# Two layers of cross-attention and feed-forward: the beta add moved ahead of the output product, and the last chunk's exponentials summed on VectorE

## The chip, the cores and the metric

One core of a Trainium2 chip. The metric is the device time of one execution in microseconds (us); the time of a kernel is the median of several runs. Engines are named as in the profile: PE (TensorE, matmuls), PEld (its weight loads), DVE (VectorE), ACT (ScalarE), POOL (GpSimd), SP (SyncE, which issues transfers here).

## The reference, cut to what matters

There are 8 batches of 112 tokens of width 512, and a context of 375 rows for each batch. Four steps follow each other, each added to the tokens: a one-head attention over the context, a quantized feed-forward, an attention with 16 heads of width 32, and a feed-forward with integer weights. The change lies in the third:

```python
scores = clip(q @ k.T / sqrt(32), -50, 50);  masked positions get -50
probs  = exp(scores) / sum(exp(scores))           # over the 375 rows of the context
ctx    = probs @ v                                # 16 heads side by side: 512 wide
delta  = rs * (ctx @ Wo.T + bo)
delta  = (delta - mean(delta)) / sqrt(var(delta) + 1e-5) * ln_gamma + ln_beta
x      = x + delta
```

Then `x` is normalized again (the kernel's "4" names) and goes into the last feed-forward.

## The kernel before, in words

The 896 tokens lie in SBUF as 7 tiles of 128 (`xs[i]`). Up to about 235 us the kernel does the first attention, the first feed-forward and the queries of the second attention. From about 235 to 396 us it runs the second attention, and after that the last feed-forward. In the stage that is changed the order on every engine is the order in which the code emits: nothing is reordered, and each engine waits in place for what its next instruction needs.

The stage is a loop over 8 batches `b` and, in each, 3 chunks `c` of 125 context rows. One step does the following.

- `scores(b, c)`: 16 small matmuls (L905) into four PSUM banks named "s", one for each of four groups of heads. DVE clips each bank into an SBUF tile (L910, four instructions of 125x448) and ACT takes the exponential in place (L911). The pool of banks has four, so the next scores wait for these clips.
- `fill(1)`: one step of the keys (L194) or values (L203) of a later batch, one to three steps a batch. It goes into one of only two PSUM buffers of the pool `ps_mm`; ACT evicts it (L197, L205). The product with Wo and the transposes of `transpose4` take their buffers from the same pool in turn.
- `sums(...)` of the step before: 16 matmuls of the exponentials with the values (L931) into "num". With the last chunk come 8 matmuls with a matrix of ones (L926) into "den", which holds the denominators: four over the first chunk's tiles, to which the second chunk's have been added, and four over the last chunk's tiles. ACT copies both out (L937, L938).
- `add(b)`, at chunk 2: the second chunk's exponentials are added into the first chunk's tiles, four tiles of 125x448 (L897). For batches 0 to 6 POOL does it, for batch 7 DVE. There are three sets of four tiles, and batch `b`, chunk `c` uses set `(b + c) % 3`.
- `convert_integers()`, at most steps: one or two pieces of the integer weights of the last feed-forward, which a transfer brought into one of two buffers "raw", are squared by ACT (L880, for a check of their range) and converted by POOL (L882). Then SP issues the next loads (L869) into the buffers that become free.
- `divide(b - 1)`, at chunk 1, on DVE: reciprocals of the denominators (L947) and products with them (L948).

The second half of a tile's work, for tile `i = b - 2`, is spread over batches `b` and `b + 1`. At chunk 2 of batch `b` (from batch 2 on):

- `write4(b - 3)` on DVE (L837), for the tile before, whose four transposes on PE (L844) follow the product;
- `project_product(i)`: 8 records of matmuls with Wo (L803) into a buffer of `ps_mm`;
- `project_begin(i)`: DVE adds the bias out of PSUM (L809), takes mean and variance (L143, L144, L812), and POOL computes a reciprocal root in small steps (`rsqrt_pool`, L105 to L109), scales it (L815) and adds beta to the tokens (L816). DVE applies gamma (L817).

At chunk 0 of the next batch, after its clips, ACT and DVE evict the transposes (L847, L848), and `project_end(i)` adds the update to the tokens on DVE (L822, which needs L815's factor and L816's tokens), takes the moments (L824 to L827) and starts another `rsqrt_pool`.

In chunk 2 of a batch the emitted order is: POOL's `add(b)`, `convert_integers()`, scores with clips and exponentials, a fill, `sums` of chunk 1, `write4`, the product, `project_begin`, the transposes.

A last tile's `project(6)` stands early in the last feed-forward, whose gate and up products are the matmuls of L1045.

Of the kernel before, what the change touches and what calls it, by code (L numbers as in the profile page):

```python
# [36 lines left out]
B, T, D = 8, 112, 512  # L37
KC = D // P
S2, CK = 375, 125
NCK = S2 // CK  # L40
# [5 lines left out]
NR = P // HD  # L46
# [24 lines left out]
def two_layers(ctx: ExitStack, tc: tile.TileContext, x, ctxT, ctxN, mask0, mask1, w1, w2, w3,  # L71
               wq, wk, wv, wo, bq, bk, bv, bo, gamma, beta, rscale,
               wg, sg, wu, su, wd, sd, out):
    nc = tc.nc
# [22 lines left out]
    xs = [tokens[:, i, :] for i in range(NT)]  # L97

    def rsqrt_pool(v, y, name):

        bits = stat.tile([P, 1], I32, name=f"{name}_b")
        nc.vector.tensor_scalar(bits, v.bitcast(I32), 1, None, ALU.logical_shift_right)
        nc.vector.tensor_scalar(y.bitcast(I32), bits, -1.0, RSQRT, ALU.mult, ALU.add)
        h = stat.tile([P, 1], F32, name=f"{name}_h")
        nc.gpsimd.tensor_scalar(h, v, -0.5, 1.0, ALU.mult, ALU.mult)  # L105
        t = stat.tile([P, 1], F32, name=f"{name}_t")
        for _ in range(3):
            nc.gpsimd.tensor_scalar(t, y, y, h, ALU.mult, ALU.mult)
            nc.gpsimd.tensor_scalar(y, t, 1.5, y, ALU.add, ALU.mult)  # L109
# [26 lines left out]
    def moments(srcs, name):  # L136

        r = srcs[0].shape[0]
        mv = small[-1].tile([P, len(srcs), nc.vector.BN_AGGR_DIM], F32, name=f"{name}_mv",
                             bufs=buffers(name))[:r]  # L140
        for j, src in enumerate(srcs):
            bn = small[-1].tile([P, nc.vector.BN_STATS_DIM], F32, name="bn", bufs=4)[:r]
            nc.vector.bn_stats(bn, src)  # L143
            nc.vector.bn_aggr(mv[:, j, :], bn)  # L144
        return mv
# [15 lines left out]
    def load(pool, src, shape, name, queue=nc.sync, dtype=F32):  # L161
        t = pool.tile(shape, dtype, name=name)
        queue.dma_start(out=t, in_=src)
        return t
# [550 lines left out]
    beta_s = load(tailp, beta.to_broadcast([P, D]), [P, D], "beta", nc.gpsimd)  # L715
# [82 lines left out]
    updates = {}  # L798

    def project_product(i):  # L800
        updates[i] = ps = ps_mm.tile([P, D], F32, name="mm")
        for kc in range(KC):
            nc.tensor.matmul(ps, lhsT=qT[:, kc, i * P:(i + 1) * P], rhs=wo_s[:, kc, :],  # L803
                             start=(kc == 0), stop=(kc == KC - 1))

    def project_begin(i):

        d = tailp.tile([P, D], F32, name="d", bufs=2)
        nc.vector.tensor_add(d, updates[i], bo_s)  # L809
        mv = moments([d], "ln3")  # L810
        var = stat.tile([P, 1], F32, name="ln3_var")
        nc.vector.tensor_scalar(var, mv[:, 0, 1:2], rs2, LN_EPS, ALU.mult, ALU.add)  # L812
        f = stat.tile([P, 1], F32, name="ln3_f")
        rsqrt_pool(var, f, "ln3")
        nc.gpsimd.tensor_scalar(f, f, rs, 1.0, ALU.mult, ALU.mult)  # L815
        nc.gpsimd.tensor_add(xs[i], xs[i], beta_s)  # L816
        nc.vector.scalar_tensor_tensor(d, d, mv[:, 0, 0:1], gamma_s, ALU.subtract, ALU.mult)  # L817
        updates[i] = d, f

# [31 lines left out]
    with tc.tile_pool(name="work2", bufs=1, side="right") as work2, \  # L851
# [14 lines left out]
        def load_integers(count):  # L866
            for w, which, half, c, n in todo[:count]:
                raw = work2.tile([P, PIECE], I32, name="raw", bufs=2)[:, :n]
                nc.sync.dma_start(out=raw, in_=w[:, c:c + n])  # L869
                loaded.append((raw, which, half, c - HALVES[which][half], n))  # L870
            del todo[:count]

        def convert_integers():
            for raw, which, half, c, n in loaded:
# [15 lines left out]
        sets = [[work2.tile([P, KC, T], F32, name=f"e{i}{r}") for r in range(NR)]  # L890
                for i in range(NCK)]

        def add(b):
            add = (nc.gpsimd if b in ADD_POOL else nc.vector).tensor_add
            for r in range(NR):
                e, e1 = (sets[(b + c) % NCK][r][:CK] for c in range(2))
                add(e, e, e1)  # L897

        def scores(b, c):
            kT = kvs_of[b][0]  # L900
            ss = [ps_s.tile([CK, KC, T], F32, name="s") for r in range(NR)]
            for dc in range(KC):
                for r in range(NR):
                    rows = slice(r * HD, (r + 1) * HD)
                    nc.tensor.matmul(ss[r][:, dc, :], lhsT=kT[rows, dc, c * CK:(c + 1) * CK],  # L905
                                     rhs=qT[rows, dc, b * T:(b + 1) * T], start=True, stop=True)
            es = sets[(b + c) % NCK]
            for r in range(NR):
                e = es[r][:CK]
                nc.vector.tensor_scalar(e, ss[r], upper[:, c, b:b + 1], -CLIP, ALU.min, ALU.max)  # L910
                nc.scalar.activation(e, e, AF.Exp, scale=SC1)  # L911
            return es
# [3 lines left out]
        def sums(b, c, es):  # L916
            if c == 0:
                sums.num = ps_av.tile([P, KC, T], F32, name="num")
            num = sums.num
            v = kvs_of[b][1]  # L920
            if c == NCK - 1:
                den = ps_av.tile([P, KC, T], F32, name="den")
                added = sets[b % NCK]
                for k, of in enumerate((added, es)):
                    for r in range(NR):
                        nc.tensor.matmul(den[r * HD:(r + 1) * HD], lhsT=ones[:CK, :HD],  # L926
                                         rhs=of[r][:CK], start=(k == 0), stop=(k == 1))
            for dc in range(KC):
                for r in range(NR):
                    head = slice((4 * dc + r) * HD, (4 * dc + r + 1) * HD)  # L930
                    nc.tensor.matmul(num[r * HD:(r + 1) * HD, dc, :], lhsT=v[:, c, head],  # L931
                                     rhs=es[r][:CK, dc, :], start=(c == 0 and dc == 0),
                                     stop=(c == NCK - 1 and dc == KC - 1))
            if c == NCK - 1:

                rden = added[0]
                nc.scalar.copy(rden, den)  # L937
                nc.scalar.copy(qT[:, :, b * T:(b + 1) * T], num)  # L938
                rdens[b] = rden
# [10 lines left out]

        STEPS = [3, 3, 3, 3, 2, 3, 3, 3]
        ADD_POOL = range(B - 1)
        last, rdens, later = None, {}, []
        folding = fold_bias()
        counts = list(due.values())
        load_integers(counts.pop(0))
        for b in range(B):
            for c in range(NCK):
                if c == 2 and b in ADD_POOL:
                    add(b)  # L960
                if (b, c) in due:
                    convert_integers()
                    if counts:
                        load_integers(counts.pop(0))
                es = scores(b, c)
                if c == 2 and b not in ADD_POOL:
                    add(b)
                if c < STEPS[b]:
                    fill(1)
                if c == NCK - 1:  # L970
                    sums(*last)
                if (b, c) == (B - 1, NCK - 1):
                    over = tailp.tile([P, 29], F32, name="over")
                    nc.gpsimd.tensor_scalar(over, squares, WIDE, 1.0, ALU.is_gt, ALU.mult)
                if b == 0 and c > 0:
                    next(folding)
                if c == 0:
                    while later:
                        later.pop()()
                    if b >= 3:  # L980
                        project_end(b - 3)
                elif c == 1 and b >= 1:
                    divide(b - 1)
                elif c == 2:
                    turned = 3 <= b < 3 + GROUPS[0][1]
                    if turned:
                        write4(b - 3)
                    if b >= 2:
                        project_product(b - 2)
                    if b == B - 1:  # L990

                        hits = ps_s.tile([1, 29], F32, name="s")
                        nc.tensor.matmul(hits, lhsT=ones[:, :1], rhs=over, start=True, stop=True)
                        wide = tailp.tile([1, 1], I32, name="wide")
                        nc.vector.tensor_reduce(wide, hits, AX.X, ALU.max)
                    if b >= 2:
                        project_begin(b - 2)
                    if turned:
                        later.append(transpose4(b - 3, ps_mm, "mm"))
                if last and c < NCK - 1:  # L1000
                    sums(*last)
                last = b, c, es
# [202 lines left out]
```

## Time and profile before

| | before |
|---|---|
| median of 3 runs | 516.82 us (516.54 to 517.11) |
| the profiled execution's own time | 516.34 us |
| its span, first to last instruction | 514.2 us |
| granted TensorE clock, mean | 0.997 |
| PE busy | 502.5 us, 98% |
| DVE busy | 337.2 us, 66% |
| ACT busy | 252.8 us, 49% |
| POOL busy | 134.4 us, 26% |

Busy time by engine in the stage that is changed, from the trace in windows of about one batch each:

| window (us) | length | PE | DVE | ACT | POOL |
|---|---|---|---|---|---|
| 267.9 to 290 | 22.1 | 22.10 | 12.07 | 10.63 | 5.96 |
| 290 to 309 | 19.0 | 18.87 | 16.94 | 11.36 | 13.32 |
| 309 to 330 | 21.0 | 20.23 | 19.17 | 11.67 | 11.02 |
| 330 to 350 | 20.0 | 20.00 | 16.15 | 12.16 | 13.39 |
| 350 to 372 | 22.0 | 21.89 | 18.90 | 13.89 | 13.95 |
| 372 to 394 | 22.0 | 22.00 | 18.03 | 13.95 | 10.76 |

How to read it: shares are averages, and an engine off the chain of work that ends last may idle at no cost. PE's busy time counts a matmul from when it began to when its end is modelled, with waits inside a group of matmuls included. A line such as "L809 DVE" means line 809 of the kernel before. In a timeline the columns are start, length, engine, line, operation, output <- input, shape, how many were merged, and in brackets the idle time of the engine before it and what released it. One fp32 matmul leaves two records in the trace.

### The profile page before, as it was taken

What the parts mean: (1) busy time and instruction counts of PE and PEld (TensorE: products, weight loads), DVE (VectorE), ACT (ScalarE), POOL (GpSimd) and SP (SyncE); (2) the same over time, 40 slices, a digit from 0 to 9 for tenths busy, and PEclk for the clock granted to TensorE, in tenths of its full rate; (3) what the DMA queues carried; (4) which work ended last, traced back from release to release, by engine and by line L of the source; (5) the groups of instructions that cost most, each with busy time, mean ns of one, the idle gap of its engine ahead of it and who ended that gap; (6) DMA issues with size and microseconds to landing.
All of it is one profiled execution on the core that took longest, in us unless ns stands there. A gap on an engine that the chain in (4) does not pass through costs nothing.

```text
span 514.2 us, 8868 instructions
## 1 busy us (share of the span) xinstructions
PE 502.5 (98%) x3402; PEld 315.8 (61%) x3402; DVE 337.2 (66%) x815; ACT 252.8 (49%) x438; POOL 134.4 (26%) x221
## 2 busy tenths in 40 slices
PE   9999999999999999999999999999999999999995
PEld 6445554455545455696565565555555788889984
DVE  3552548767798987965676688986897753334432
ACT  0326656857565666236675366465665233103310
POOL 0000121110111064211551475674754430000000
PEclk9999999999999999999999999999999999999998
DMA  8998795200120100122421112012320000010001
GB/s 241 347 407 326 268 324 205 80 18 0 61 82 1 60 2 0 45 101 61 162 68 51 62 52 62 3 53 62 98 69 13 20 1 1 20 42 20 1 20 48
DMA packets 13489, 45.77 MB, mean 89 GB/s; under 512 B 2097, under 2 KB 3392, under 8 KB 12288
## 3 DMA queue, kind: packets, MB, share of 16 engines
q1 hardware_dynamic: 11888, 41.43, 23.5%
q0 software_dynamic: 1248, 3.70, 2.2%
q8 instruction: 29, 0.48, 0.4%
q14 instruction: 20, 0.16, 0.1%
q10 hardware_dynamic: 304, 0.01, 0.0%
HBM read 41.46 MB, written 1.84 MB: 84 GB/s over the span
## 4 chain that ended last, share of the span: by engine, by line
PE 47%; DVE 6%; POOL 2%; ACT 1%; DMA 1%; issue 1%; DVEq 0%; POOLq 0%; ACTq 0%
PE s L1045 14%; PE mm L203 8%; PE down L1067 7%; PE mm L803 3%; PE s L905 3%; PE num L931 2%; PE mm L194 2%; DVE e L910 2%; PE den L926 2%; PE mm L740 1%; PE mm L738 1%; DMA raw<-in_wd_dram 1%; PE s L744 1%; DVE e L947 1%; ACT e L911 1%
## 5 line engine op out<-in xcount | busy, mean ns | idle before, releaser
L203 PE MATMUL mm<-wv,cT 128*125 128x512 f32 x192 | 87.6, 599 | 0.0
L194 PE MATMUL mm<-cT,wk 128*128 128x375 f32 x256 | 87.3, 485 | 0.0
L1045 PE MATMUL s<-h4T,w 128*128 128x512 f32 (+1 forms) x352 | 72.6, 367 | 0.2 <-PE num L931 0.2
L1045 PEld LDWEIGHTS s<-h4T,w 128*128 128x128 f32 x352 | 63.5, 188 | 8.8 <-PE num L931 0.4
L910 DVE TENSOR_SCALAR e<-s,upper 125x448 f32<-125x448 f32 x96 | 59.0, 677 | 14.7 <-PE s L905 13.9
L911 ACT ACTIVATE e<-e 125x448 f32<-125x448 f32 x96 | 51.6, 570 | 27.8 <-DVE e L910 27.3
L194 PEld LDWEIGHTS mm<-cT,wk 128*128 128x128 f32 x256 | 46.8, 190 | 27.6 <-issue 1.0
L203 PEld LDWEIGHTS mm<-wv,cT 128*125 128x125 f32 x192 | 34.5, 187 | 38.0 <-issue 36.4
L897 POOL TENSOR_TENSOR e<-e,e 125x448 f32<-125x448 f32 x28 | 33.1, 1213 | 15.8 <-PE num L931 15.8
L1067 PE MATMUL down<-w,gu 128*128 128x512 f32 (+1 forms) x176 | 37.0, 367 | 0.0
L541 PE MATMUL mm<-w_q,q_qT 128*128 128x512 fp8e4 (+1 forms) x168 | 34.8, 361 | 0.8 <-DVE tokens L583 0.4
L439 POOL DMA_DIRECT2D tokens<-x x14 | 10.7, 768 | 90.3 <-DVE x L433 63.0
L1067 PEld LDWEIGHTS down<-w,gu 128*128 128x128 f32 x176 | 29.8, 188 | 5.7
L880 ACT ACTIVATE w<-raw,zero_point 128x640 fp32r<-128x640 int32 (+2 forms) x29 | 22.6, 781 | 20.4 <-DMA raw<-in_wd_dram 9.2
L1053 ACT CAST gu<-gu 128x512 fp32r<-128x512 f32 (+1 forms) x22 | 12.5, 568 | 39.6 <-DVE gu L1051 39.6
L570 POOL TENSOR_SCALAR q<-gu 128x704 bf16<-128x704 f32 x14 | 10.8, 790 | 79.8 <-ACT gu L567 79.8
L882 POOL TENSOR_SCALAR w<-raw 128x640 fp32r<-128x640 int32 (+2 forms) x29 | 20.7, 724 | 36.0 <-ACT w L880 35.8
L905 PE MATMUL s<-qT,kv 32*125 32x112 f32 x768 | 29.4, 280 | 0.6 <-DVE qT L748 0.3
L1051 DVE SCALAR_TENSOR_TENSOR gu<-s,su,gu 128x512 f32<-128x512 f32 (+1 forms) x22 | 15.1, 684 | 21.8 <-PE s L1045 20.6
L905 PEld LDWEIGHTS s<-qT,kv 32*125 32x125 f32 x768 | 24.5, 183 | 7.1 <-issue 5.8
L541 PEld LDWEIGHTS <-q_qT 128*128 128x128 bf16 x168 | 16.3, 98 | 19.7 <-issue 2.5
L931 PEld LDWEIGHTS num<-e,kv 125*32 125x32 f32 x768 | 18.4, 110 | 13.6 <-issue 7.9
(238 smaller groups left out, 798.6 us busy)
## 6 DMA issues: line engine op xcount, KB each, us to landing
cT<-in_ctxT_dram SPq DMA_DIRECT2D x13, 750.0 KB, 6.1
raw<-in_w_dram SPq DMA_DIRECT2D x6, 1408.0 KB, 20.3
cN<-in_ctxN_dram SPq DMA_DIRECT2D x8, 768.0 KB, 4.5
raw<-in_wg_dram SPq DMA_DIRECT2D x8, 320.0 KB, 3.0
raw<-in_wu_dram SPq DMA_DIRECT2D x8, 320.0 KB, 2.9
raw<-in_wd_dram SPq DMA_DIRECT2D x8, 320.0 KB, 3.1
out_dram<-d SPq DMA_DIRECT2D x6, 256.0 KB, 2.0
wk<-in_wk_dram SPq DMA_DIRECT2D x4, 256.0 KB, 4.9
```

The source lines that it names most:

```text
L194: nc.tensor.matmul(ps[dc], lhsT=wk_s[:, kc, dc * P:(dc + 1) * P], rhs=cT[:, kc, :], start=(kc == 0), stop=(kc == KC - 1))
L203: nc.tensor.matmul(ps, lhsT=cT[:, kc, c * CK:(c + 1) * CK], rhs=wv_s[:, kc, :], start=(kc == 0), stop=(kc == KC - 1))
L541: nc.tensor.matmul(ps[:, :n], lhsT=qT[:, kc, :], rhs=w[:, kc * H + n0:kc * H + n0 + n], start=(kc == 0), stop=(kc == KC - 1))
L880: nc.scalar.activation(t, raw, AF.Square, bias=zero_point, accum_out=squares[:, k:k + 1])
L882: nc.gpsimd.tensor_scalar(t, raw, -128.0, 1.0, ALU.add, ALU.mult)
L897: add(e, e, e1)
L905: nc.tensor.matmul(ss[r][:, dc, :], lhsT=kT[rows, dc, c * CK:(c + 1) * CK], rhs=qT[rows, dc, b * T:(b + 1) * T], start=True, stop=True)
L910: nc.vector.tensor_scalar(e, ss[r], upper[:, c, b:b + 1], -CLIP, ALU.min, ALU.max)
L911: nc.scalar.activation(e, e, AF.Exp, scale=SC1)
L931: nc.tensor.matmul(num[r * HD:(r + 1) * HD, dc, :], lhsT=v[:, c, head], rhs=es[r][:CK, dc, :], start=(c == 0 and dc == 0), stop=(c == NCK ...
L1045: nc.tensor.matmul(ps[:, :n], lhsT=w[:, c:c + P], rhs=h4T[k][:, kc, :n], start=(kc == 0 and k == 0), stop=(kc == KC - 1 and k == 1))
L1067: nc.tensor.matmul(ps, lhsT=gus[k][:, hc, j * P:(j + 1) * P], rhs=w[:, c + n0:c + n0 + n], start=(hc == 0 and k == 0), stop=(hc == HC - 1 ...
```

## The change

Two edits. First, the POOL instruction that adds beta to a tile of tokens moves from `project_begin`, where it followed the reciprocal root, to the head of `project_product`, so that it stands on POOL ahead of the reciprocal root and is issued while the product runs.

Second, in batches 2 to 6 DVE adds the last chunk's exponentials into the tiles that hold the first two chunks' sum (`add_last`, four instructions of 125x448 for each batch, ahead of `project_begin`), and the four ones-matmuls over the last chunk's tiles are left out: the denominator is then one set of four matmuls instead of two. Batches 0, 1 and 7 keep theirs.

```diff
     def project_product(i):
+
+        nc.gpsimd.tensor_add(xs[i], xs[i], beta_s)
         updates[i] = ps = ps_mm.tile([P, D], F32, name="mm")
...
         nc.gpsimd.tensor_scalar(f, f, rs, 1.0, ALU.mult, ALU.mult)
-        nc.gpsimd.tensor_add(xs[i], xs[i], beta_s)
         nc.vector.scalar_tensor_tensor(d, d, mv[:, 0, 0:1], gamma_s, ALU.subtract, ALU.mult)
...
+        def add_last(b):
+            for r in range(NR):
+                e, e1 = (sets[(b + c) % NCK][r][:CK] for c in (0, NCK - 1))
+                nc.vector.tensor_add(e, e, e1)
...
-                for k, of in enumerate((added, es)):
+                parts = (added,) if b in ADD_LAST else (added, es)
+                for k, of in enumerate(parts):
                     for r in range(NR):
                         nc.tensor.matmul(den[r * HD:(r + 1) * HD], lhsT=ones[:CK, :HD],
-                                         rhs=of[r][:CK], start=(k == 0), stop=(k == 1))
+                                         rhs=of[r][:CK], start=(k == 0),
+                                         stop=(k == len(parts) - 1))
...
         ADD_POOL = range(B - 1)
+        ADD_LAST = range(2, B - 1)
...
+                    if b in ADD_LAST:
+                        add_last(b)
                     if b >= 2:
                         project_begin(b - 2)
```

## The prediction

> **What bounds the kernel now.** I read the page's busy shares, then the chain that ended last in order of time, then each engine's timeline through the second attention (234.8 to 395.6 us), where both edits lie. The page:
>
> ```profile
> PE 502.5 (98%) x3402; PEld 315.8 (61%) x3402; DVE 337.2 (66%) x815; ACT 252.8 (49%) x438; POOL 134.4 (26%) x221
> ```
>
> TensorE has work nearly always, so a matmul taken away could be time won; but a PE that waits for a bank inside a group of matmuls still counts as busy here, and the chain (start, length, what) shows where it does:
>
> ```profile
> 295.41 1.24 POOL tokens L816
> 296.67 0.76 DVE tokens L822
> ...
> 299.47 1.87 DVE e L910 x3
> 301.38 1.12 PE s L905 x26
> ...
> 328.61 0.61 PE mm L844 x4
> ...
> 333.92 1.64 PE den L926 x16
> ...
> 363.38 3.66 DMA raw<-in_wd_dram
> ...
> 369.86 0.47 ACT kv L197
> 370.37 0.66 PE mm L844 x4
> ```
>
> Read: at 295.4 the beta add on POOL holds up DVE, DVE's clips then free the score banks late, and PE resumes at 301.38. PE is held again at 328.6, and at 370.4 by a transfer, the exponentials behind it and an eviction. VectorE's timeline (start, length; idle before in brackets):
>
> ```profile
> 308.98 0.53 DVE L837 TENSOR_SCALAR d<-tokens,mv,rstd 128x512 f32<-128x512 f32 x1
> 309.80 0.69 DVE L809 TENSOR_TENSOR d<-mm,bo 128x512 f32<-128x512 f32 x1 [0.28 <-PE mm L803]
> 316.57 0.88 DVE L822 SCALAR_TENSOR_TENSOR tokens<-d,ln_f,tokens 128x512 f32<-128x512 f32 x1 [0.88 <-POOL tokens L816]
> 327.91 0.54 DVE L837 TENSOR_SCALAR d<-tokens,mv,rstd 128x512 f32<-128x512 f32 x1
> 388.35 2.22 DVE L897 TENSOR_TENSOR e<-e,e 125x448 f32<-125x448 f32 x4
> ```
>
> From 296.67 to 328.45 DVE has only those two pauses: in batches 3 and 4 it is as tight as PE. TensorE and GpSimd at the places that matter:
>
> ```profile
> 311.84 2.79 PE L194 MATMUL mm<-cT,wk 128*128 128x375 f32 x8
> 328.59 0.63 PE L844 MATMUL mm<-ident,d 128*128 128x128 f32 x4 [0.34 <-ACT e L911]
> 330.22 3.70 PE L203 MATMUL mm<-wv,cT 128*125 128x512 f32 x8
> ```
>
> ```profile
> 389.38 1.78 POOL L882 TENSOR_SCALAR w<-raw 128x640 fp32r<-128x640 int32 x1 [1.78 <-ACT w L880]
> ```
>
> The pause at 328.59 is put down to an exponential, but the transposes read what L837 wrote until 328.45: it is DVE. The L882, 0.726 us by its median, took 1.78 because it began inside the four adds of 388.35 and ended (391.16) 0.6 after them (390.57): the two engines exclude each other.
>
> **The change, part by part.** "+" is later, "-" earlier than in this trace.
>
> Denominator. Batches 2 to 6 drop 4 of 8 ones-matmuls. 16 records (two per matmul) cost the chain 1.64 us, so 8 cost 0.82: five times that, 4.1 us, is all that PE can win.
>
> Adds. 20 on DVE, at 2.22 us per four (388.35): 11.1 us of DVE. They stand ahead of L809, and behind L809 wait the moments, POOL's rsqrt, the next batch's clips and L822. L809 also frees the product's PSUM buffer, and `ps_mm` has two: the fill after next (311.84 and 330.22 above) needs that one.
>
> Port. An add waits for the POOL instruction under way: from nothing up to one whole beta add (1.285 median). Two rows show such waits: L948 on 128x320 took 1.43 at 305.06 beside POOL's adds, 0.81 at 363.98. For the adds I take about 0.4 a batch, the rest of one L882 or beta add.
>
> Beta add. The same instruction (1.285 median) goes ahead of the rsqrt. L822 no longer waits for it: 1.2 at 296.67, about 0.9 at 316.57, 335.13, 357.07 and 377.06 (DVE is done with L848 that long before). Its new cover is the product, 3.63 us in which POOL has at most two L882; uncovered, it would cost its 1.285. L882 of the next chunk 0 now follows L815 directly, and so do the transfers that reuse its buffers. SP, ACT and all other orders stay.
>
> The walk, batch by batch:
>
> Batch 2: the exponentials end at 286.6, the adds at about 288.5, ahead of L809 (289.91): hidden by DVE's idle 3.94. Denominator -0.8. L822 goes at 295.45 instead of 296.67; DVE follows without a gap, so L837 of batch 3 is at -1.2, and PE's stall at 301.38 shrinks with it: PE -1.2.
>
> Batch 3: beta sits on POOL until 308.9, the adds run 308.8 to 310.75, so L809 is at +0.95 (309.80). PE would reach the fill (311.84) at 310.6 and waits for that L809 to end, 311.5: -0.35. Denominator to -1.15; the scores of (4,1) then wait for clips that are at +0.95: -0.85. L822: +0.95 - 0.9 = about 0. So L837 in batch 4 is at about +0.1, and the transposes of 328.59 wait for it: PE at +0.1. All that was won is gone.
>
> Batch 4: adds 328.6 to 330.55, L809 (328.36) at +2.2. The fill of 330.22 waits until 331.3: PE +1.05, less the denominator: +0.25. L822: +2.2 - 0.9 = +1.3.
>
> Batch 5: half a microsecond of port waits in the division makes the clips +1.7; L837 ends at 349.25, beta at 349.9, the adds at 351.65. L809 had waited 2.73 us for PE (350.29), which takes up most: +1.4. The fill of 351.69 waits until 352.4, PE +0.7, denominator to -0.1; L822 +1.4 - 0.9 = +0.5.
>
> Batch 6: from that L822 lead POOL's rsqrt, L882, the transfer of 363.38, L880, the exponentials and the eviction of 369.86 to the transposes of 370.37: PE +0.5. Its adds put L809 at +1.4 (ends 372.4), the fill comes at 372.5: no wait. Denominator: 0.5 - 0.82 = -0.3.
>
> Batch 7: no new adds; DVE +0.4. The range test of L993 needs L974 (391.62 in the trace, PE there at 392.90), so 0.4 is covered. From 395.6 PE runs on and -0.3 is carried to the end. `project(6)` gets its beta earlier, hidden by 144 matmuls.
>
> In short: if s is the shift of L809 in batch 5, the end moves by s - 0.9 - 0.82. With s = 1.4 that is -0.3; without port waits in batch 5 s is 0.9 and it is -0.8. The port wait is known no better than that, so I take the middle, -0.5. The profiled execution is 516.34 us, 514.2 of it span; 516.34 - 0.5 = 515.84. The median of the runs, 516.82, lies 0.48 higher, so 516.3 on the scale of the medians. 0.2% or 1.03 us is about what a measurement can tell from no change.
>
> Here a rule speaks against the change: the Trainium skill, "SBUF — State Buffer", section "SBUF: two separate sides", has the pair that DVE and GpSimd share given to an instruction for its whole length, the loser fully blocked. By it the pair could change hands after each add; the row above shows POOL kept out over two adds in a row instead. Were it handed over each time, the sum would be that of the second rival.
>
> **The rivals.**
>
> First, faster: PE's bound holds and DVE finds room. For it: DVE idles 3.94, 2.73 and 1.23 us before L809 in batches 2, 5 and 6, and the beta wait is 5.0 us in total; also the 0.4 to 0.6 us port waits may fall away as the phases move (the L948 of 302.29, 0.67, and that of 305.06 lost about 1 us to them, beside 0.29 and 0.81 for the same sizes at 365.69 and 363.98). Against it: batches 3 and 4 have no such idle time. With s = 0 it gives -0.9 - 0.82 = -1.7, 515.1; the far end is -2.9, if the chain of 363.38 came 1.2 earlier still, a whole beta add.
>
> Second, slower: POOL gets in between the adds. Place: batches 3, 5 and 6, where two L882 and the beta add are queued on POOL just then. Price: 2 x 0.726 + 1.285 = 2.7 us instead of 0.4, so s = 1.4 + 2.3 = 3.7 and the end +2.0, 518.8. It decides from s = 1.7, and is seen as slower from s = 2.75. For it: the exponentials land one by one, 0.47 to 0.59 apart, so adds that wait for them leave gaps. Against it: in 388.35 no gap let POOL in.
>
> That the change doesn't do what it says can be set aside: the built program has 20 matmuls less and 20 DVE adds more, with the beta add ahead of L105 on POOL.
>
> **How the numbers follow.** Forecast (s from 0.5 to 2.8; -1.2 to +1.1) 0.48; first rival 0.32; second 0.20. Faster by over 0.2%: the first rival and a little of the forecast, 0.34. Slower: the second, and walks in which L809's lateness adds up in batches 3 and 4, 0.22. Same: 0.44. The range leaves out the far fifth: from -2.1 (514.7) to +1.4 (518.2); the forecast's own is 515.6 to 517.9.
>
> **What would show it.** In the new profile: den with 88 records instead of 128; 20 adds on DVE of 0.6 to 1.1 us; L822 without a POOL wait. Right, if L809 of batch 4 starts some 2 us later relative to L837 and the fill after it (330.22) stands idle or lengthened by 1 us. Wrong towards faster, if batches 3 to 5 have no PE pause above 0.3; wrong towards slower, if four adds span over 3.5 us with L882 or the beta add between them, or if the transfer of 363.38 comes over 1 us late.

## The result, and the profile after

The changed kernel takes 518.81 us (median of 7 runs, 517.88 to 521.14) against 516.82 us before (7 runs). The ratio is 1.0042, with a 95% interval of 1.0025 to 1.0058: slower by 2.2 us (0.42% of 516.82). The forecast was 516.3 with a range up to 518.2; the measured time lies outside it, and of the rivals it is nearest to the second.

The profiled execution of the changed kernel took 518.22 us, 516.4 of it span. The shares on its page:

```profile
PE 499.5 (97%) x3362; PEld 314.7 (61%) x3362; DVE 352.2 (68%) x835; ACT 251.7 (49%) x438; POOL 134.0 (26%) x221
```

PE lost the 40 records that the halved denominators were to save (3402 before) and is busy 3.0 us less, yet the span is 2.2 us longer. DVE is busy 15.0 us more, where the 20 adds at 2.22 us per four are 11.1. Most of the rest is waiting inside instructions, which then last longer. DVE's timeline of the changed kernel, where line 838 is the write of the normalized tile (837 before), 903 the new adds and 811 the add of the bias out of PSUM (809 before):

```profile
308.19 1.41 DVE L838 TENSOR_SCALAR d<-tokens,mv,rstd 128x512 f32<-128x512 f32 x1
309.53 2.22 DVE L903 TENSOR_TENSOR e<-e,e 125x448 f32<-125x448 f32 x4
311.67 0.68 DVE L811 TENSOR_TENSOR d<-mm,bo 128x512 f32<-128x512 f32 x1
...
328.99 0.54 DVE L838 TENSOR_SCALAR d<-tokens,mv,rstd 128x512 f32<-128x512 f32 x1
329.44 2.23 DVE L903 TENSOR_TENSOR e<-e,e 125x448 f32<-125x448 f32 x4
...
349.68 1.60 DVE L838 TENSOR_SCALAR d<-tokens,mv,rstd 128x512 f32<-128x512 f32 x1
351.20 2.22 DVE L903 TENSOR_TENSOR e<-e,e 125x448 f32<-125x448 f32 x4
353.35 0.68 DVE L811 TENSOR_TENSOR d<-mm,bo 128x512 f32<-128x512 f32 x1
...
371.04 3.67 DVE L903 TENSOR_TENSOR e<-e,e 125x448 f32<-125x448 f32 x4
374.64 0.68 DVE L811 TENSOR_TENSOR d<-mm,bo 128x512 f32<-128x512 f32 x1
```

The write took 0.53 to 0.59 us before; in batches 3 and 5 it now takes 1.41 and 1.60. For batch 5 the kernel before has:

```profile
346.98 0.59 DVE L837 TENSOR_SCALAR d<-tokens,mv,rstd 128x512 f32<-128x512 f32 x1
```

The adds of batch 6 span 3.67 instead of 2.2. POOL's timeline of the same kernel shows what ran there, beta's add at its new line 802, in batches 3 to 6:

```profile
308.05 1.27 POOL L802 TENSOR_TENSOR tokens<-tokens,beta 128x512 f32<-128x512 f32 x1
...
327.45 1.27 POOL L802 TENSOR_TENSOR tokens<-tokens,beta 128x512 f32<-128x512 f32 x1
...
349.73 1.27 POOL L802 TENSOR_TENSOR tokens<-tokens,beta 128x512 f32<-128x512 f32 x1
...
371.54 1.62 POOL L802 TENSOR_TENSOR tokens<-tokens,beta 128x512 f32<-128x512 f32 x1
```

At 308.05 beta's add begins 0.14 us before the write and ends at 309.32; the write ends 0.28 later. At 371.54 it begins within the run of adds. In batch 4 beta's add is done at 328.72, before the write, which takes 0.54. POOL is not made late by beta's add: it then idles 3.4 to 5.2 us in every batch from 2 to 7 until DVE brings the variance.

The adds of batch 7, which are on DVE in both kernels, show it once more, without an idle moment between them: 3.31 us here, 2.22 before.

```profile
391.44 3.31 DVE L898 TENSOR_TENSOR e<-e,e 125x448 f32<-125x448 f32 x4
392.36 1.37 POOL L802 TENSOR_TENSOR tokens<-tokens,beta 128x512 f32<-128x512 f32 x1
```

One of the four begins at 392.52, beside beta's add, and takes 1.69 instead of 0.62. This costs nothing: DVE idles 1.00 us behind it. TensorE's timeline shows where PE pays (idle before in brackets, then what ended it):

```profile
309.75 0.63 PE L845 MATMUL mm<-ident,d 128*128 128x128 f32 x4 [0.80 <-DVE d L838]
...
312.40 2.80 PE L194 MATMUL mm<-cT,wk 128*128 128x375 f32 x8 [0.95 <-DVE d L811]
...
329.67 0.63 PE L845 MATMUL mm<-ident,d 128*128 128x128 f32 x4 [1.42 <-ACT e L917]
...
332.32 3.70 PE L203 MATMUL mm<-wv,cT 128*125 128x512 f32 x8 [0.95 <-DVE d L811]
...
354.08 2.80 PE L194 MATMUL mm<-cT,wk 128*128 128x375 f32 x8 [0.95 <-DVE d L811]
...
375.37 3.70 PE L203 MATMUL mm<-wv,cT 128*125 128x512 f32 x8 [0.80 <-DVE d L811]
```

Four fills wait for the product's PSUM buffer, 3.65 us in all, and the transposes of batches 3 and 4 wait for the written tile (the second pause is put down to an exponential, but the write ends at 329.53, just ahead of them). Before, the longest of these pauses was 0.43:

```profile
310.19 0.66 PE L844 MATMUL mm<-ident,d 128*128 128x128 f32 x4 [0.43 <-ACT kv L197]
```

### The profile page after: what moved, and what is told of

It is laid out like the page before. It is cut to its first block, busy times and chain, and to the rows that moved or that the text cites. A ratio compares the mean times of both kernels' runs of the same rounds, so it can differ in the third digit from the quotient of the medians.

```text
span 516.4 us, 8799 instructions
## 1 busy us (share of the span) xinstructions
PE 499.5 (97%) x3362; PEld 314.7 (61%) x3362; DVE 352.2 (68%) x835; ACT 251.7 (49%) x438; POOL 134.0 (26%) x221
## 4 chain that ended last, share of the span: by engine, by line
PE 42%; DVE 11%; issue 2%; DMA 2%; ACT 1%; POOL 1%; DVEq 0%; POOLq 0%; ACTq 0%
PE s L1056 14%; PE down L1078 7%; PE mm L203 6%; DVE e L916 3%; PE s L911 2%; PE mm L194 2%; PE mm L805 2%; PE num L939 2%; DVE e L955 2%; DVE e L903 2%; PE den L933 1%; PE mm L740 1%; PE mm L738 1%; PE s L744 1%; ACT e L917 1%
## 5 line engine op out<-in xcount | busy, mean ns | idle before, releaser
L883 POOL TENSOR_SCALAR w<-raw 128x640 fp32r<-128x640 int32 (+2 forms) x29 | 19.5, 682 | 34.4 <-ACT w L881 34.0
```

The costliest lines, as they stand in the source:

```text
L883: nc.gpsimd.tensor_scalar(t, raw, -128.0, 1.0, ALU.add, ALU.mult)
```

## The experiments

All are timed against the kernel before on the same chip; "ratio" is that to the kernel before, with its 95% interval. The runs were spread over several chips, so they are compared with each other by their ratios. Four explanations are told apart. A: the collision, beta's add on POOL holds up what DVE does beside it. B: the load, the adds cost DVE time wherever beta is. C: the buffer, PE waits for the product's PSUM buffer. D: DVE is as tight as PE in batches 3 and 4, so that adds can't pay there. The first four runs take the two edits apart.

**Beta moved, no adds.**

```diff
-        ADD_LAST = range(2, B - 1)
+        ADD_LAST = ()
```

> The changed kernel with the new adds taken out again (all batches sum the denominator with 8 matmuls); only beta's add stands at its new place. Theory A, the collision: in the changed kernel's trace the beta add runs on POOL just when DVE writes the normalized tile, and that write took 1.41 and 1.60 us in batches 3 and 5 instead of 0.54, so the new place costs 0.9 to 1.1 us of DVE there. Then this kernel shows writes of 1.2 to 1.6 us, yet with no adds DVE has idle time behind them in batch 5, so it should end 0.5 to 2 us ahead of the kernel before. Theory B, the load: the adds alone make the loss, wherever beta is; then the same, 1 to 2.5 us ahead, with L822's waits of 5.0 us gone. Both die if this is slower than before.

Measured: 515.36 us, 0.9972 (0.9962 to 0.9982), 1.4 us faster. The first edit by itself wins. But DVE's timeline of this kernel shows the write held up here too, in batch 4 as well, without any new add beside it:

```profile
308.29 1.41 DVE L838 TENSOR_SCALAR d<-tokens,mv,rstd 128x512 f32<-128x512 f32 x1
...
327.39 1.12 DVE L838 TENSOR_SCALAR d<-tokens,mv,rstd 128x512 f32<-128x512 f32 x1
```

**Adds, beta at its old place.**

```diff
     def project_product(i):
-        nc.gpsimd.tensor_add(xs[i], xs[i], beta_s)
...
         nc.gpsimd.tensor_scalar(f, f, rs, 1.0, ALU.mult, ALU.mult)
+        nc.gpsimd.tensor_add(xs[i], xs[i], beta_s)
```

> The changed kernel with beta's add put back behind the reciprocal root; the 20 new adds stay. Theory A: the write of the normalized tile is back at 0.54 to 0.59 us, but the tokens wait for beta again, about 0.9 us a batch; the two nearly cancel, so 518.5 to 520, about like the changed kernel. Theory B, load alone: the wait for beta comes on top, so the changed kernel's +2.2 plus 0.9 for each of the batches where DVE is tight (3, 4, 5, 6): 520 to 522.

Measured: 520.44 us, 1.0082 (1.0069 to 1.0095), 4.2 us slower. The writes are back at 0.53 to 0.57, and the tokens wait for beta again, 1.45 and then 0.85 or 0.86 us a time. So the time alone favours theory B, load. It does not exclude A: neither theory had said how much of the load is a wait. Set beside each other, the runs also say which edit loses: beta's new place is better than the old one with the adds (1.0042 against 1.0082) and without them (0.9972 against 1), and the adds cost 4.2 us with beta at its old place and 3.6 at its new one.

**The eviction ahead of the adds.**

```diff
-                    if b in ADD_LAST:
-                        add_last(b)
                     if b >= 2:
-                        project_begin(b - 2)
+                        project_begin(b - 2, (lambda: add_last(b)) if b in ADD_LAST else None)
...
         nc.vector.tensor_add(d, updates[i], bo_s)
+        if between is not None:
+            between()
```

> The changed kernel with the four adds behind the eviction of the product (the add of the bias out of PSUM) instead of ahead of it. Theory C, the buffer: PE loses its time where a fill waits for the product's PSUM buffer, 0.95 + 0.95 + 0.95 + 0.80 us of PE idle in batches 3 to 6 of the changed kernel; with the eviction first these four waits go, and what is left of DVE's lateness shows as waits for clips and for the written tile: 515.5 to 517.5. Theory B, load: DVE has the same 11 us more ahead of the next clips, so PE waits there instead: 518 to 519.5, with the idle time ahead of the fills moved to the scores.

Measured: 519.28 us, 1.0045 (1.0032 to 1.0058), no better than the changed kernel. The fills no longer wait, as theory C says, but nothing is won: PE's timeline of this kernel has the time in the scores of batch 3, which take 2.90 us instead of 1.14 because their banks are freed late (2.70 and 2.23 in batches 4 and 6), and in the transposes:

```profile
296.00 2.90 PE L913 MATMUL s<-qT,kv 32*125 32x112 f32 x32 [0.17 <-DVE e L918]
...
332.59 0.63 PE L847 MATMUL mm<-ident,d 128*128 128x128 f32 x4 [1.41 <-ACT e L919]
```

The PSUM buffer is only where PE meets DVE's lateness, not its cause. Theory C falls.

**All betas early.** POOL had idled 9.3 us in batch 2; all seven beta adds go there.

```diff
     def project_product(i):
-        nc.gpsimd.tensor_add(xs[i], xs[i], beta_s)
...
+                if (b, c) == (2, 1):
+                    for x_tile in xs:
+                        nc.gpsimd.tensor_add(x_tile, x_tile, beta_s)
```

> The changed kernel with all seven beta adds issued on POOL in chunk 1 of batch 2, where POOL idled 9.3 us before; the new adds stay. Theory A: the writes are at 0.54 to 0.6 us, no set of four adds is over 2.9 us, and 0.9 (batch 3) and 1.0 (batch 5) us of DVE and over 1 us of batch 6 come back: 516 to 517. Theory B, load: 518 to 519, as the changed kernel, since DVE's own work is unchanged.

Measured: 515.07 us, 0.9977 (0.9965 to 0.9988). With the same 20 adds on DVE, the changed kernel's 2.2 us loss becomes a gain of 1.2, and by the ratios the adds cost 0.9 us instead of 3.6 (the kernel without them follows below). DVE's timeline of this kernel at the three places:

```profile
307.97 0.54 DVE L837 TENSOR_SCALAR d<-tokens,mv,rstd 128x512 f32<-128x512 f32 x1
...
348.56 0.54 DVE L837 TENSOR_SCALAR d<-tokens,mv,rstd 128x512 f32<-128x512 f32 x1
...
368.72 2.73 DVE L902 TENSOR_TENSOR e<-e,e 125x448 f32<-125x448 f32 x4
```

That beta's place decides is clear; that it is the collision and not the tokens' wait needed one more run.

**A POOL add that nobody waits for.** To the kernel with betas early comes an add of the same size where the changed kernel has beta's. It writes a scratch tile.

```diff
+    scratch = tailp.tile([P, D], F32, name="scratch")
...
+        if i < NT - 1:
+            nc.gpsimd.tensor_add(scratch, bo_s, beta_s)
         updates[i] = ps = ps_mm.tile([P, D], F32, name="mm")
```

> Betas early with the new adds (515.07), plus a POOL add of the same size at the place where the changed kernel has beta's: it reads the bias and beta and writes a scratch tile that nobody reads, so nobody waits for it. Theory A (DVE and POOL exclude each other at their memory access): the write of the normalized tile is 1.4 to 1.6 us again in batches 3 and 5, the adds of batch 6 over 3 us, and the time is back at the changed kernel's, 518 to 519. If instead the data of beta's add mattered (a wait for the tokens), nothing changes: 515 to 515.5.

Measured: 519.01 us, 1.0058 (1.0038 to 1.0078). The whole loss is back, from an instruction whose result nobody reads. DVE's timeline of this kernel, with the write at line 840 and the adds at 905:

```profile
307.78 1.41 DVE L840 TENSOR_SCALAR d<-tokens,mv,rstd 128x512 f32<-128x512 f32 x1
...
349.26 1.42 DVE L840 TENSOR_SCALAR d<-tokens,mv,rstd 128x512 f32<-128x512 f32 x1
...
370.31 3.80 DVE L905 TENSOR_TENSOR e<-e,e 125x448 f32<-125x448 f32 x4
```

One other way to lose time remains, that the extra add makes POOL's own next work late. POOL's timeline of this kernel excludes it: behind the add of 307.64 to 308.90 POOL idles 4.31 us for DVE (3.4 to 5.2 in batches 2 to 7).

```profile
313.21 0.19 POOL L105 TENSOR_SCALAR ln_h<-ln_var 128x1 f32<-128x1 f32 x1 [4.31 <-DVE ln_var L816]
```

Theory A is shown: six POOL adds that only stand in DVE's way cost 0.81% by the ratios (1.0058 against 0.9977), 4.2 us. The six runs spread from 517.54 to 521.63; between the two profiled executions, 517.54 and 514.77, the cost is 2.8. PE's pauses in these two agree with that: from the transposes of batch 3 to the fill of batch 6 they sum to 6.36 us here and 3.63 with betas early alone, and of the 2.7 between, 0.9 lie in batch 3, nothing in batch 4, 0.8 in batch 5 and 1.0 in batch 6.

**What the adds are worth with beta out of the way.** Betas early, no adds:

```diff
-        ADD_LAST = range(2, B - 1)
+        ADD_LAST = ()
```

> All seven beta adds in POOL's pause of batch 2, no new adds on DVE, all denominators by 8 matmuls. It tells what the adds and the halved denominators are worth when beta is out of their way, since the same with the adds took 515.07 (0.9977 of before). Theory A, the collision alone made the loss: the adds then pay with PE time, so this is slower than 515.07, up to 3 us: 515.5 to 517. Theory D, DVE is as tight as PE: the adds give nothing even with a free port, so this is within 1 us of 515.07 or below it: 514 to 515.5.

Measured: 514.16 us, 0.9960 (0.9947 to 0.9972). The adds in five batches gain nothing on top of it (0.9977); they seem to lose 0.9 us, though the two intervals overlap. This is theory D's answer: DVE is as tight as PE.

**The price of the matmuls by themselves.** Betas early, no adds, and the denominators of batches 2 to 6 cover the last chunk alone:

```diff
-                parts = (added,) if b in ADD_LAST else (added, es)
+                parts = (es,) if b in ADD_LAST else (added, es)
...
-                    if b in ADD_LAST:
-                        add_last(b)
```

> Betas early; in batches 2 to 6 the four matmuls over the first two chunks' sum are left out of the denominators (they then cover the last chunk alone), and there are no new adds. It prices the 4.1 us of PE by themselves, with DVE unburdened. If a TensorE microsecond in this stage is a microsecond of the end: 3 to 4 us below the kernel with betas early and full denominators. If DVE or the transfers of the integer weights hold PE anyway, less than 2 us. Theory D expects something in between, 1.5 to 3.5 us, since the stage is held by DVE in batches 3 and 4 and by transfers in batch 6.

Measured: 512.00 us, 0.9913 (0.9901 to 0.9926). Against 0.9960 that is 0.47%, 2.4 us; the two intervals leave about 1.5 to 3.4. On PE's timelines of this kernel and of the one before it, each halved denominator brings the matmuls behind it 0.75 us forward: 3.8 in five batches, where the prediction had 4.1. Of that 1.1 is lost again by the transposes, 0.8 in batch 3 and 0.3 in batch 6, though DVE gets no new work. In batch 3 PE now waits for an eviction of a fill by ACT:

```profile
308.90 0.66 PE L844 MATMUL mm<-ident,d 128*128 128x128 f32 x4 [0.43 <-ACT kv L197]
```

**Which batches.** Betas early with adds in batches 3 and 4 alone, and the changed kernel with adds in 2, 5 and 6 alone:

```diff
-        ADD_LAST = range(2, B - 1)
+        ADD_LAST = (3, 4)
```

> Betas early, new adds only in batches 3 and 4, where DVE had no idle time but 0.28 us ahead of the eviction. Theory D (DVE is as tight as PE there): each set of adds holds DVE for 2.2 us and gives PE 0.82, so this is slower than betas early without adds (514.16, 0.9960 of before): by 1 to 2.5 us, 515 to 516.5. If adds are paid only by the collision with POOL, it is faster than 514.16, by up to 1.6.

Measured: 516.50 us, 1.0012 (0.9996 to 1.0029), which is 0.52% or 2.7 us above no adds at all. The 12 runs spread from 515.54 to 519.44; by the medians it is 2.3 us. In batches 3 and 4 the adds lose even with beta away, at the upper end of what was expected: PE's timeline has the transposes 1.42 late and the fill behind them 0.95.

```profile
328.71 0.63 PE L844 MATMUL mm<-ident,d 128*128 128x128 f32 x4 [1.42 <-ACT e L916]
331.36 3.70 PE L203 MATMUL mm<-wv,cT 128*125 128x512 f32 x8 [0.95 <-DVE d L810]
```

```diff
-        ADD_LAST = range(2, B - 1)
+        ADD_LAST = (2, 5, 6)
```

> The changed kernel, beta at its place under the product, with adds only in batches 2, 5 and 6. Theory A and D together: batches 3 and 4 cost 0.9 and 0.6 us by the written tile alone, as with beta moved and no adds (0.9972 of before); in batch 5 the idle 2.7 us take the write's wait and part of the adds, in batch 6 the beta add still gets between the adds. So 514.5 to 516.5, 2 to 4 us below the changed kernel. If the loss sits in batches 5 and 6, it stays at 517.5 to 519.

Measured: 515.79 us, 0.9986 (0.9977 to 0.9995), as A and D together expect. On DVE's timeline of this kernel beta's add now gets between the adds of batch 5 as well:

```profile
347.14 3.81 DVE L903 TENSOR_TENSOR e<-e,e 125x448 f32<-125x448 f32 x4
```

**Versions that beat both kernels.** Betas early, and adds only where DVE has idle time: batches 2, 5 and 6; these and batch 0; and 0, 2 and 5.

```diff
-        ADD_LAST = range(2, B - 1)
+        ADD_LAST = (2, 5, 6)
```

> Betas early, and the new adds and halved denominators only in batches 2, 5 and 6, where DVE idled 3.94, 2.73 and 1.23 us ahead of the product's eviction before. Theory D: PE saves 3 x 0.82 = 2.5 us where DVE has room and loses nothing in batches 3 and 4: 0.5 to 2 us below the kernel with all five, 513 to 514.5. Theory A: room on DVE doesn't matter once beta is away, so it loses the 1.6 us of two batches against the kernel with all five: 515.5 to 517.

> Betas early, adds in batches 0, 2, 5 and 6. In batch 0 DVE idles too and the denominator comes 4 us after the exponentials: 0.8 us below adds in 2, 5 and 6 (513.25, 0.9953 of before), 512 to 513. If PE waits for DVE's adds in batch 0, no gain: 513 to 514.

> Betas early, adds in batches 0, 2 and 5. Against adds in 0, 2, 5 and 6 it tells what the adds of batch 6 are worth, which wait for exponentials that a transfer holds up (2.73 us for four instead of 2.22). If batch 6 pays: 0.3 to 0.8 us slower than with it, 512.8 to 513.8. If its lateness costs as much as it saves: the same within 0.3.

Measured: 513.25 us, 0.9953 (0.9936 to 0.9969); with batch 0, 511.98 us, 0.9911 (0.9897 to 0.9925); without batch 6, 513.08 us, 0.9930 (0.9918 to 0.9943). The best is 4.6 us ahead of the kernel before. Batch 6 seems to pay, 1.1 us by the medians, with its adds at 2.73; the two intervals just overlap. Batch 0 was expected to give 0.8 us and the medians differ by 1.3; the evictions of batch 2 (L810) come 0.93 us earlier with it (289.09 against 290.02), 0.18 of which the two traces already differ at 235 us. That leaves the 0.75 of one halved denominator; what lies above it is not explained.

## Why the prediction was wrong

The two profiled executions are not level where the change begins: the scores of batch 2, chunk 2 start at 281.02 in the changed kernel and at 280.57 before. The table takes this 0.45 off and puts the walk's shifts beside the measured ones.

| event | predicted | measured |
|---|---|---|
| eviction of the product, batch 3 | +0.95 | +1.4 |
| fill behind it | -0.35 | +0.1 |
| written tile, batch 4 | +0.1 | +0.6 |
| eviction, batch 4 | +2.2 | +2.8 |
| update of the tokens, from L809 of batch 4 | +1.3 | +1.8 |
| eviction, batch 5 (s) | +1.4 | +2.6 |
| eviction, batch 6 | +1.4 | +3.9 |
| first matmul of the last feed-forward | -0.3 | +2.2 |

The path of the walk was right: the adds ahead of the eviction, the fill that waits for the PSUM buffer, DVE without idle time in batches 3 and 4, and a beta add that no longer holds up the tokens (its waits shrank from 5.0 us to 0.2). The sign that it named for this came: in batch 4 the eviction starts 2.59 us behind the write, 0.45 before, and the fill stands idle for 0.95. So did one that it named for "wrong towards slower": four adds over 3.5 us with the beta add between them, in batch 6. What was mis-sized is what beta's add holds up at its new place. The walk ends at -0.3 and the measured start of the last feed-forward at +2.2; by the table 0.5 of the 2.5 between arise in batch 3, 0.7 in batch 5 and 1.3 in batch 6.

First, "Its new cover is the product" was the step that failed. Beside the tokens' wait, beta's add was charged only as a port wait of the new adds, "about 0.4 a batch". What it runs beside is the write of the normalized tile, which the walk moved along at 0.54 in every batch. It took 0.87 more in batch 3 and 1.06 more in batch 5. The prediction had the exclusion of the two engines in its own fence and applied it to instructions with two inputs in SBUF, the adds and the products of the division. The write has one. A slip of the sum comes on top in batch 3: the four adds pass in 1.95 us there (308.8 to 310.75), where its own row has 2.22 and the new trace 2.14 from the first add to the eviction.

Here the skill was read too narrowly. The Trainium skill, "SBUF — State Buffer", section "Who interferes with whom", names `tensor_scalar` among the DVE operations that can enter a mode with two ports and then contend with GpSimd, whatever issues first blocking the other. The write is one, and 1.41 to 1.60 us beside a POOL add against 0.54 agree with it; which mode it ran in no run here shows.

Second, the port wait of the adds, "about 0.4 a batch", held in batches 3 to 5 as a bound (2.22 and 2.23 us, with no wait of their own). In batch 6 it was 1.4. A transfer came late there (ACT waited 3.33 us for it), and with it the two conversions and the beta add queued behind them on POOL: the first add waited for a conversion, beta's add went next, and the second add waited for that. The second rival had this price and the place right for batch 6 alone; in batches 3 and 5 the write took the wait and the adds ran unbroken, with nothing left on POOL beside them. What spoke for it, adds that wait for exponentials and leave gaps, was not needed: in batch 6 the exponentials were done 0.10 to 1.76 us before the adds that read them began. What spoke against it, that POOL was kept out over two adds at 388.35, is one row; in batches 6 and 7 of the changed kernel POOL got in between adds that followed each other without a gap. That the second rival gave 518.8 is part coincidence.

Third, "the end moves by s - 0.9 - 0.82" gives +0.9 with the measured s of 2.6, which lies inside the forecast's own 0.5 to 2.8. The other 1.3 is batch 6, which the formula treats as free: 0.8 of it is the fill's wait of 0.80 us, where none was expected; the rest is not divided further. The 0.82 itself measures 0.75.

The first rival is refuted in its mechanism. DVE's idle time in batches 2, 5 and 6 does take the adds of these batches (513.25 against 514.16 without adds, though those intervals overlap); batches 3 and 4 lose what they gain, as the run with these two alone shows.

The forecast's bare walk is not far off once the collision is out: with betas early the same adds give -1.2 us, where -0.5 was predicted, inside the forecast's own -1.2 to +1.1 only at its edge. And the 4.1 us that "PE can win" are 3.8 by the rows, of which 2.4 can be had.

What stays open is how much the written tile and batch 6 would each cost alone: PE's pauses divide the loss (0.9, 0.8 and 1.0 us in batches 3, 5 and 6 of the run with the scratch add), but no run removed one of them. Open too is what decides whether a waiting POOL instruction gets in between two adds.

## What to carry to other kernels

An instruction that is moved to an engine with idle time is paid for by whatever runs beside it at the new place: list the neighbours on the engine that shares its access, not only its readers. Here the same seven beta adds were worth 1.4 us under the product, 2.1 in a pause where DVE had little to do, and beside the new vector adds six such adds that nobody read cost 2.8 to 4.2. Trade matmuls for vector work batch by batch, where the vector engine idles: in all five the adds gained nothing, in four chosen ones they took the kernel to 511.98.

## What the runs showed of the hardware that was not expected

- A 128x512 fp32 tensor_scalar on DVE with one tile in SBUF as input waits for a POOL add under way: 1.12 to 1.60 us instead of 0.54. It ended 0.28 us after the POOL instruction.
- Four DVE adds of 125x448 took 2.21 to 2.23 us with no POOL add beside them, and 3.30 to 3.81 when one was queued on POOL while they ran: it went between two adds that followed each other without idle time. Keeping them free of gaps did not keep POOL out (batches 6 and 7 of the changed kernel); in the kernel before one POOL conversion was kept out over two of them (1.78 us instead of 0.726).
- These waits stand inside the length of the waiting instruction and not in the idle time before it, as the write of 1.41 us shows: they are found by comparing the same instruction's lengths.
- PE time by itself was worth 0.6 of its length in this stage (2.4 of 3.8 us), although PE is busy 98% of the span.
